# Four-head attention layer: logits row spread over partitions by DMA, mask built beside the first batch, one clock for all batches

## The chip, the cores and the metric

The kernel runs on one core of one Trainium2 chip. The time is the device time of one execution in microseconds. Before the change it is 3026.18 us (median of 3 runs, 3023.26 to 3026.87). The profiled execution has a span of 3030.3 us.

## What is computed

32 graphs (batches) of 512 nodes with 256 features share one 512 x 512 adjacency matrix. Four layers follow one another, each on the normed input and added to it. Cut to what matters here, with the four-head layer in full:

```
for layer in 0..3:
    h = max(layernorm(x), 0);  x = x + gat(h)

layers 0, 1:  Wh = h @ W;  e[i,j] = leaky(s_i[i] + s_j[j]);  masked softmax over j;  att @ Wh
layer 2 (four heads of 64 features):
    Wh = (h @ W).reshape(B, N, 4, 64)
    e[i,j,h] = leaky(s_src[i,h] + s_dst[j,h]), alpha = 0.2, masked by adj
    alpha = softmax over j;  out[i,h,:] = sum_j alpha[i,j,h] Wh[j,h,:];  elu
layer 3:  mlp1 -> unmasked gat of width 512 -> mlp2 -> masked gat of width 256, with residuals
```

The kernel uses exp(leaky(a + b)) = exp(b) exp(alpha a) max(R[i], T[j]) with R and T exponentials of one node each, and what depends on the row i alone drops out of the softmax. So the unnormed weights of a head are, transposed, w[j, i] = max(R[i], T[j]) x mask[j, i]. T is a column per partition; R must stand as a row of 512 on every partition.

## The kernel before

All 32 batches are unrolled. Four streams (`NS = 4`) work on batches b, b+1, b+2, b+3 side by side; stream i takes batches i, i+4, and so on (`stream`, L709). Each batch is a generator that yields a due time wherever it may be interrupted; the loop at L722 always advances the stream with the earliest due time. `after_us` (L62) makes the due time: the stream's time, plus `STRETCH` times the matmul cycles of this step, plus `SLOW` (1.5) times the microseconds given, times `pace`. Streams start `LEAD = 75` due microseconds apart. A fifth generator, `setup` (L213), is advanced every 4 due microseconds and prepares the weights of later layers. The due times fix the order in which instructions are written; a list scheduler may still move independent instructions of an engine past one another, unless `tc.keep_in_program_order` holds one in place. After that each engine's queue runs in order.

For the last four batches `pace` is 1.15, 1.025, 0.9 and 0.775 (L712), so that the streams, which run 75 due microseconds apart, are drawn together at the end.

`weights` (L335) makes w for one head: four TensorE transposes (L72) of R's column, broadcast to 128 x 128, against the identity fill a PSUM bank with R on every partition; then four DVE instructions (L343) of 128 x 512 take max(R, T) x mask into the SBUF tile w. [...] `layer2` (L424) makes the values v of all heads, begins head 0, and then for each head begins the next one (`begin`, L443), yields, and aggregates: 16 matmuls of 65 columns (L458), a reciprocal and a multiplication into the tile ya (L461). Layers 0, 1 and 3 use `weights` once each.

Layer 3's unmasked attention is done by sorting (`sort_attend`, L527): rows are scattered to DRAM by GpSimd (L571), read back in order by SyncE (L578), summed, written as a table (L611, L612) and gathered (L619). Only the last batch uses `attend` instead, by matmuls. SyncE's queue thus carries the sort's reads and writes, the loads of x (L89) and the outputs (L678).

The mask (L190 to L202) is made before the first batch: adj is loaded (1 MB), DVE compares it (L191), GpSimd sets the diagonal (L192), TensorE turns it with 16 transposes and ACT copies it to bf16.

Of the kernel before, what the change touches and what calls it, by code (L numbers as in the profile page):

```python
# [19 lines left out]
FP = mybir.dt.float32  # L20
# [4 lines left out]
OP = mybir.AluOpType  # L25
AX = mybir.AxisListType

EPS = 1.0e-5
P = 128
# [2 lines left out]
TINY = 1.0e-30  # L32
CYCLES = 2400.0


@with_exitstack
def fast(ctx, tc, flag, x, adj, w0, a0, w1, a1, w2, a2, mlp1_w, mlp1_b, mlp2_w, mlp2_b,
         w_fc, a_fc, w_hand, a_hand, out):
    nc = tc.nc
    B, N, F = x.shape  # L40
    NT = N // P
# [3 lines left out]
    NH = a2.shape[0]  # L45
    D = F // NH
    NS = 4
    LEAD = 75.0
    SLOW = 1.5
    STRETCH = 2.0  # L50

    const = ctx.enter_context(tc.tile_pool(name="const", bufs=1))
    work = ctx.enter_context(tc.tile_pool(name="work", bufs=2))
    psum = ctx.enter_context(tc.tile_pool(name="psum", bufs=1, space=bass.MemoryType.PSUM))
    dram = ctx.enter_context(tc.tile_pool(name="dram", bufs=1, space=bass.MemoryType.DRAM))

    turn = [0]
    begun = [0.0]
    spent = [0.0]
    pace = [1.0] * NS  # L60

    def after_us(us):  # L62

        return begun[0] + pace[turn[0]] * (STRETCH * spent[0] / CYCLES + SLOW * us)

    def matmul(p, w, x, **flags):
        spent[0] += 4 * max(x.shape[-1], P)
        nc.tensor.matmul(p, w, x, **flags)  # L68

    def transpose(p, x, i):  # L70
        spent[0] += 2 * P
        nc.tensor.transpose(p, x, i)  # L72

    def bank():
        return psum.tile([P, N], FP, tag=f"b{turn[0]}", name="b", bufs=8 // NS)
# [3 lines left out]
    ident = const.tile([P, P], FP, name="ident")  # L79
# [23 lines left out]
    def scale_a(t, alpha):  # L103
        nc.vector.tensor_scalar_mul(t[:, :, 1:2], t[:, :, 0:1], alpha - 1.0)
        nc.vector.tensor_scalar_mul(t[:, :, 2:3], t[:, :, 2:3], 1.0 - alpha)
# [25 lines left out]
    def finish_w(fetched, alpha):  # L131
        t, a_cols = fetched

        def block(k, f):
            c = f * P + (3 if f * P >= F else 0)
            return t[:, k, c:c + P]

        scale_a(a_cols, alpha)
        for k in range(t.shape[1]):
            project(t[:, k, F:F + 3], block, k, a_cols)  # L140
            yield
# [4 lines left out]
    adj_sb = work.tile([P, NT, N], I32, tag="w", name="adj", bufs=4)  # L146
# [10 lines left out]
    for h in range(NH):  # L157
        t, r = divmod(h * D, P)
# [27 lines left out]
    for _ in finish_w(fetched0, 0.2):  # L186
        pass


    own = work.tile([P, NT, N], FP, tag="w", name="own", bufs=4)  # L190
    nc.vector.tensor_scalar(own, adj_sb, 0.0, None, op0=OP.is_gt)  # L191
    nc.gpsimd.affine_select(  # L192
        out=own, in_=own, pattern=[[P, NT], [-1, N]], base=0, channel_multiplier=1,
        compare_op=OP.not_equal, fill=1.0,
    )
    maskT = const.tile([P, NT, N], BF, name="maskT")
    for j in range(NT):
        turn[0] = j % NS
        p = bank()
        for t in range(NT):  # L200
            transpose(p[:, t * P:(t + 1) * P], own[:, t, j * P:(j + 1) * P], ident)
        nc.scalar.copy(maskT[:, j, :], p)  # L202

    before = const.tile([P, P], FP, name="before")
    after = const.tile([P, P], FP, name="after")
    band = const.tile([P, 2 * N - P], BF, name="band")
    differ = const.tile([P, 2], FP, name="differ")
# [4 lines left out]

    def setup():  # L213

        yield from finish_w(fetched1, 0.01)


        nc.vector.tensor_reduce(differ[:, 0:1], adj_sb, AX.XY, OP.min)
        nc.vector.tensor_scalar(differ[:, 0:1], differ[:, 0:1], 0.0, None, op0=OP.is_lt)
        least = small([1], "rden")  # L220
        nc.vector.tensor_reduce(least, diag, AX.X, OP.min)
        nc.vector.tensor_scalar(differ[:, 1:2], least, 0.0, None, op0=OP.is_le)
        nc.vector.tensor_copy(W2[:, :, :, :D], raw2.rearrange("p k (h d) -> p k h d", d=D))
        nc.vector.tensor_scalar_mul(A2v[:, :, 1:2], A2v[:, :, 0:1], -0.8)
        nc.vector.tensor_scalar_mul(A2v[:, :, 2:3], A2v[:, :, 2:3], 0.8)
        for k in range(KF):
            project(W2[:, k, :, D:], lambda k, f: raw2[:, k, f * P:(f + 1) * P], k, A2)
            yield
        yield from finish_w(fetched3, 0.2)

        for tri, sign in ((before, 1), (after, -1)):
            nc.vector.memset(tri, 1.0)
            nc.gpsimd.affine_select(
                out=tri, in_=tri, pattern=[[sign, P]], base=0, channel_multiplier=-sign,
                compare_op=OP.is_gt, fill=0.0,
            )
        ties = work.tile([P, 2 * N - P], FP, tag="w", name="ties", bufs=4)
        nc.vector.memset(ties, TINY)
        nc.gpsimd.affine_select(
            out=ties, in_=ties, pattern=[[-1, 2 * N - P]], base=N - P, channel_multiplier=1,  # L240
            compare_op=OP.is_gt, fill=0.0,
        )
        nc.vector.tensor_copy(band, ties)
        yield
        yield from finish_w(fetched4, 0.2)
# [3 lines left out]
    def small(shape, name):  # L249
        return work.tile([P] + shape, FP, tag=name, name=name, bufs=2 * NS)  # L250
# [81 lines left out]
            yield after_us(0.9 if f == ft - 1 else 0)  # L332
        return o

    def weights(r_col, t_col, masked=True):  # L335

        r = bank()
        for t in range(NT):
            transpose(r[:, t * P:(t + 1) * P], r_col(t).to_broadcast([P, P]), ident)
        wt = work.tile([P, NT, N], FP, tag="w", name="w", bufs=4)  # L340
        for j in range(NT):
            if masked:
                nc.vector.scalar_tensor_tensor(  # L343
                    wt[:, j, :], r, t_col(j), maskT[:, j, :], op0=OP.max, op1=OP.mult
                )
            else:
                nc.vector.tensor_scalar(wt[:, j, :], r, t_col(j), None, op0=OP.max)  # L347
        return wt

    def pair(tag="y"):  # L350
        return work.tile([P, 2, F], FP, tag=tag, name=tag, bufs=3)
# [72 lines left out]
    def layer2(xt, xn, rs, when):  # L424
        hT = yield from turned(xn, when)
        v = work.tile([P, NT, NH, CH], FP, tag="v", name="v2", bufs=4)
        for t in range(NT):
            ps = bank()
            for k in range(KF):
                matmul(  # L430
                    ps[:, :NH * CH], hT[:, k, t * P:(t + 1) * P], W2[:, k, :, :], start=(k == 0), stop=(k == KF - 1)
                )
            pv = ps[:, :NH * CH].rearrange("p (h c) -> p h c", c=CH)
            nc.scalar.activation(v[:, t, :, D:], pv[:, :, D:], AF.Exp, scale=rs[:, t:t + 1])
            nc.vector.scalar_tensor_tensor(
                v[:, t, :, :D], pv[:, :, :D], rs[:, t:t + 1], v[:, t, :, D:D + 1].to_broadcast([P, NH, D]),
                op0=OP.mult, op1=OP.mult,
            )
            yield after_us(0 if t + 1 < NT else 1)
        ya = work.tile([P, NT, F], FP, tag="y4", name="y4", bufs=2)  # L440
        wts = []

        def begin(h):  # L443
            wts.append(weights(lambda t: v[:, t, h, D + 2:D + 3], lambda j: v[:, j, h, D + 1:D + 2]))
            return after_us(3.2)

        when = begin(0)
        note(v.rearrange("p t h c -> p (t h) c")[:, :, D:])
        yield after_us(1)
        for h in range(NH):  # L450
            last = when
            if h + 1 < NH:
                when = begin(h + 1)
            yield last
            wt = wts[h]
            p = bank()
            for t in range(NT):
                aggregate(p[:, t * (D + 1):(t + 1) * (D + 1)], wt, t, lambda j: v[:, j, h, :D + 1])  # L458
            pv = p[:, :NT * (D + 1)].rearrange("p (t c) -> p t c", c=D + 1)
            r = reciprocal(pv[:, :, D:])  # L460
            nc.vector.tensor_tensor(  # L461
                ya[:, :, h * D:(h + 1) * D], pv[:, :, :D], r.to_broadcast([P, NT, D]), op=OP.mult
            )
            if h % 2:
                c = slice((h - 1) * D, (h + 1) * D)
                y = ya[:, :, c]
                q = pair("q").rearrange("p a (b f) -> p (a b) f", f=2 * D)
                nc.scalar.activation(q, y, AF.Exp)
                nc.scalar.activation(y, y, AF.Relu)
                add_elu(xt[:, :, c], y, q)  # L470
            yield after_us(0)
        xn, rs = new_xn(), small([NT], "rs")
        for t0 in range(0, NT, 2):
            norm(xt, xn, rs, t0, False)
        yield after_us(7)
        return xn, rs, after_us(2)
# [231 lines left out]

    def stream(first):  # L709
        for b in range(first, B, NS):  # L710

            if b >= B - NS:  # L712
                pace[first] = 1.15 - (NS - B + b) / (2 * NS)
            yield from batch(b)


# [1 line left out]
    ready = {i: i * LEAD for i in range(NS)}  # L718
    streams = [stream(i) for i in range(NS)]
    early = setup()  # L720
    ready[NS] = 0.0
    while ready:  # L722
        i = min(ready, key=ready.get)
        if i == NS:
# [20 lines left out]
    p = bank()  # L745
# [437 lines left out]
```

## Time and profile before

| Quantity | Value |
|---|---|
| time, median of 3 | 3026.18 us |
| TensorE busy (matmul / weight load) | 2924.8 / 2368.3 us |
| DVE, ACT, GpSimd busy | 2269.9, 1489.6, 470.2 us |
| transposes that write R in layers 0 to 3 (b <- ident, v) | 896, mean 274 ns |
| w instructions on DVE (L343) | 896, mean 743 ns |
| mean DMA rate | 81 GB/s |
| first output sent / output of batch 27 sent | 289.9 / 2749.5 us |

Busy time is the time in which an engine has an instruction running. TensorE's matmuls are pipelined: a record is longer than the distance from one start to the next, so a queue of them is measured by its starts. A wait line names an engine's instruction, what released it, the total, the number of times, and the longest. "SPq" is SyncE's queue, which issues transfers. A stretch is a window in microseconds from the span's start.

### The profile page before, as it was taken

The numbers are of one execution on the slowest core, as the hardware profiler recorded it, in microseconds if no ns is written. First come the engines' busy times: TensorE is split into PE (matmuls) and PEld (weight loads), VectorE is DVE, ScalarE is ACT, GpSimd is POOL, SyncE is SP. The second block draws the span as 40 slices with busy tenths as digits, with TensorE's granted clock in tenths as the row PEclk, the third lists the DMA queues.
The fourth block names the chain that finished last, engine by engine and source line by source line (L and its number), as shares of the span: only waits on it lengthen the run. The fifth ranks groups of instructions, "written<-read, shape, count | busy, mean of one in ns | idle before, by whom it ended". The sixth has DMA issues, their size and how long they took to land. (4 is left out here: it accounts for less than half of the span.)

```text
span 3030.3 us, 43501 instructions
## 1 busy us (share of the span) xinstructions
PE 2924.8 (97%) x15529; PEld 2368.3 (78%) x15529; DVE 2269.9 (75%) x5674; ACT 1489.6 (49%) x3758; POOL 470.2 (16%) x509
## 2 busy tenths in 40 slices
PE   7999999999999999999999999999999999999897
PEld 5787887877788877788877788877888877788665
DVE  4588778777877777777778777877877877767664
ACT  3444455554455554455554455554455554454445
POOL 0011111101111201112111111101111111111111
PEclk8999999999999999999999999999999999999999
DMA  3022223222223222223232223222223222212220
GB/s 91 1 88 87 75 74 102 83 90 88 74 74 102 84 89 83 80 74 102 78 95 82 81 74 102 83 90 91 71 74 102 89 84 87 74 52 82 84 97 29
DMA packets 178685, 245.46 MB, mean 81 GB/s; under 512 B 15328, under 2 KB 153886, under 8 KB 178464
## 3 DMA queue, kind: packets, MB, share of 16 engines
q1 hardware_dynamic: 148704, 144.32, 14.9%
q0 software_dynamic: 29760, 98.30, 9.8%
q8 instruction: 125, 2.05, 0.3%
q14 instruction: 96, 0.79, 0.1%
HBM read 127.46 MB, written 115.12 MB: 80 GB/s over the span
## 5 line engine op out<-in xcount | busy, mean ns | idle before, releaser
L68 PE MATMUL b<-v,w 128*128 128x257 f32 (+1 forms) x7232 | 1225.5, 322 | 22.0 <-DVE w L343 8.6
L68 PEld LDWEIGHTS b<-v,w 128*128 128x128 f32 x7232 | 1054.2, 192 | 186.7 <-issue 51.7
L343 DVE SCALAR_TENSOR_TENSOR w<-b,v,maskT 128x512 f32<-128x512 f32 x896 | 635.7, 743 | 13.3 <-PE b L72 10.5
L68 PE MATMUL b<-WFC,oT 128*128 128x256 f32 (+1 forms) x2048 | 491.5, 380 | 0.8 <-ACT v L311 0.5
L68 PEld LDWEIGHTS b<-WFC,oT 128*128 128x128 f32 x2048 | 373.6, 189 | 50.8 <-issue 1.0
L68 PE MATMUL b<-W,hT 128*128 128x259 f32 (+1 forms) x1536 | 389.1, 391 | 9.8 <-DVE v L315 8.6
L68 PEld LDWEIGHTS b<-W,hT 128*128 128x128 f32 x1536 | 282.8, 192 | 60.2 <-DVE v L315 11.0
L571 POOL DMA_INDIRECT order<-v,at x248 | 251.1, 1013 | 462.7 <-DVE seen L298 139.9
L68 PE MATMUL b<-hT,WM 128*128 128x512 f32 x512 | 251.9, 598 | 8.2 <-ACT hT L282 7.8
L359 DVE RECIPROCAL rden<-b 128x1 f32<-128x1 f32 (+1 forms) x516 | 80.2, 163 | 233.6 <-PE b L68 230.6
L677 POOL TENSOR_TENSOR x<-x,y 128x512 f32<-128x512 f32 x64 | 81.2, 1269 | 1077.3 <-ACT y L675 980.8
L619 POOL DMA_INDIRECT g<-table,at x124 | 122.5, 988 | 790.8 <-ACT y L639 287.1
L68 PE MATMUL b<-oT,WM 128*128 128x512 f32 x512 | 232.8, 597 | 0.0
L261 DVE BATCH_NORM_STATS2 st<-x 128x6 f32<-128x256 f32 x512 | 193.2, 409 | 5.6 <-DMA x<-in_x_dram 2.7
L331 ACT ACTIVATE oT<-b,bias 128x512 f32<-128x512 f32 x128 | 87.5, 686 | 216.6 <-PE b L68 216.4
L384 DVE TENSOR_TENSOR y<-q,y 128x512 f32<-128x512 f32 x192 | 132.5, 691 | 67.1 <-ACT q L383 48.2
L72 PEld LDWEIGHTS b<-ident,xn 128*128 128x128 f32 x1024 | 125.9, 142 | 69.9 <-DVE xn L272 23.6
L493 ACT ACTIVATE v<-b,ends 128x256 f32<-128x256 f32 x256 | 120.3, 470 | 122.2 <-PE b L68 115.6
L72 PE MATMUL b<-ident,xn 128*128 128x128 f32 x1024 | 159.7, 278 | 20.4 <-DVE xn L272 8.7
L282 ACT ACTIVATE hT<-b 128x512 f32<-128x512 f32 x256 | 150.2, 593 | 40.7 <-PE b L72 39.6
L68 PEld LDWEIGHTS b<-oT,WM 128*128 128x128 f32 x512 | 95.3, 191 | 93.5 <-issue 91.4
L638 ACT ACTIVATE q<-g,rden 128x512 f32<-128x512 f32 x124 | 89.5, 722 | 145.9 <-DVE rden L359 142.7
(139 smaller groups left out, 3735.0 us busy)
## 6 DMA issues: line engine op xcount, KB each, us to landing
table<-sums SPq DMA_DIRECT2D x62, 1032.0 KB
sums<-order SPq DMA_DIRECT2D x62, 516.0 KB
x<-in_x_dram SPq DMA_DIRECT2D x32, 512.0 KB
out_dram<-x SPq DMA_DIRECT2D x64, 256.0 KB
sums<-order SPq DMA_DIRECT2D x62, 129.0 KB
order<-v,at POOLq DMA_INDIRECT x248, 2.5
g<-table,at POOLq DMA_INDIRECT x124, 4.5
adj<-in_adj_dram SPq DMA_DIRECT2D x1, 1024.0 KB
```

The costliest lines, as they stand in the source:

```text
L68: nc.tensor.matmul(p, w, x, **flags)
L72: nc.tensor.transpose(p, x, i)
L261: nc.vector.bn_stats(st[:, i, :], xt[:, t0 + i, :])
L282: nc.scalar.activation(hT[:, :, t0 * P:(t0 + 2) * P], p.rearrange("p (k n) -> p k n", k=KF), AF.Relu)
L331: nc.scalar.activation(o[:, f, :], p, AF.Relu, bias=bias[:, f:f + 1])
L343: nc.vector.scalar_tensor_tensor(wt[:, j, :], r, t_col(j), maskT[:, j, :], op0=OP.max, op1=OP.mult)
L384: nc.vector.tensor_tensor(r, q, r, op=OP.add)
L493: nc.scalar.activation(halves[c][:, t, :F], ps[:, :F], AF.Copy, scale=ends[:, t, 0:1])
L571: nc.gpsimd.indirect_dma_start(out=orders[c], out_offset=bass.IndirectOffsetOnAxis(ap=at[:, 0, t:t + 1], axis=0), in_=halves[c][:, t, :], ...
L619: nc.gpsimd.indirect_dma_start(out=g, out_offset=None, in_=table, in_offset=bass.IndirectOffsetOnAxis(ap=at[:, 1, t:t + 1], axis=0),)
L638: nc.scalar.activation(q, z, AF.Exp, scale=rd)
L677: nc.gpsimd.tensor_tensor(xr, xr, y, op=OP.add)
```

## The change

Three things are done at once.

In layer 2, only head 0 gets its R by broadcast transposes. For heads 1 to 3, four transposes of v's R columns give a 4 x 512 row tile in PSUM, ACT copies it to SBUF (a buffer of the tag q), SyncE writes it to a DRAM tile, and three reads with a partition broadcast put a row on all 128 partitions of an SBUF tile `spread` (two buffers for all streams). `weights` takes such a tile as `r` and holds the head's first w in program order. To make room, ya has one buffer instead of two. The due time after head 0 begins grows from 1 to 3.

The mask moves into `setup`, whose start moves from 0 to 7.5 due microseconds; its first transpose and the reduction of adj (L218) are held in program order.

`pace` is dropped: the last four batches have the same due times as all others.

```diff
     def after_us(us):
-        return begun[0] + pace[turn[0]] * (STRETCH * spent[0] / CYCLES + SLOW * us)
+        return begun[0] + STRETCH * spent[0] / CYCLES + SLOW * us
...
-    own = work.tile([P, NT, N], FP, tag="w", name="own", bufs=4)
-    nc.vector.tensor_scalar(own, adj_sb, 0.0, None, op0=OP.is_gt)
-    nc.gpsimd.affine_select(
...
     def setup():
+        own = work.tile([P, NT, N], FP, tag="w", name="own", bufs=4)
+        nc.vector.tensor_scalar(own, adj_sb, 0.0, None, op0=OP.is_gt)
+        nc.gpsimd.affine_select(
...
+        for j in range(NT):
+            turn[0] = NS - 1 - j % (NS - 1)
+            p = bank()
+            for t in range(NT):
+                transpose(p[:, t * P:(t + 1) * P], own[:, t, j * P:(j + 1) * P], ident, j + t == 0)
+            nc.scalar.copy(maskT[:, j, :], p)
+        turn[0] = NS - 1
+        yield
         yield from finish_w(fetched1, 0.01)
-        nc.vector.tensor_reduce(differ[:, 0:1], adj_sb, AX.XY, OP.min)
+        tc.keep_in_program_order(nc.vector.tensor_reduce(differ[:, 0:1], adj_sb, AX.XY, OP.min))
...
-    def weights(r_col, t_col, masked=True):
-        r = bank()
-        for t in range(NT):
-            transpose(r[:, t * P:(t + 1) * P], r_col(t).to_broadcast([P, P]), ident)
+    def weights(r_col, t_col, masked=True, r=None):
+        landed = r is not None
+        if not landed:
+            r = bank()
+            for t in range(NT):
+                transpose(r[:, t * P:(t + 1) * P], r_col(t).to_broadcast([P, P]), ident)
...
+                if landed and j == 0:
+                    tc.keep_in_program_order(w)
...
-        ya = work.tile([P, NT, F], FP, tag="y4", name="y4", bufs=2)
+        ya = work.tile([P, NT, F], FP, tag="y4", name="y4", bufs=1)
...
+        p = bank()
+        for t in range(NT):
+            transpose(p[:NH, t * P:(t + 1) * P], v[:, t, :, D + 2], ident)
+        row = pair("q").rearrange("p a f -> p (a f)")[:NH, :]
+        nc.scalar.copy(row, p[:NH, :])
+        row_d = dram.tile([NH, N], FP, tag="row", name="row", bufs=3)
+        nc.sync.dma_start(row_d, row)
+        spread = [None]
+        for h in range(1, NH):
+            r = work.tile([P, N], FP, tag="spread", name="spread", bufs=2)
+            nc.sync.dma_start(r, row_d[h, :].partition_broadcast(P))
+            spread.append(r)
         when = begin(0)
...
-        yield after_us(1)
+        yield after_us(3)
...
-            if b >= B - NS:
-                pace[first] = 1.15 - (NS - B + b) / (2 * NS)
...
-    ready[NS] = 0.0
+    ready[NS] = 7.5
```

More of the change, by code (lines that the diff above doesn't have):

```diff
@@ L59, in fast @@
     spent = [0.0]
-    pace = [1.0] * NS
     def after_us(us):
-        return begun[0] + pace[turn[0]] * (STRETCH * spent[0] / CYCLES + SLOW * us)
+        return begun[0] + STRETCH * spent[0] / CYCLES + SLOW * us
     def matmul(p, w, x, **flags):
@@ L68, in matmul, with transpose @@
         nc.tensor.matmul(p, w, x, **flags)
-    def transpose(p, x, i):
+    def transpose(p, x, i, tied=False):
         spent[0] += 2 * P
-        nc.tensor.transpose(p, x, i)
+        instruction = nc.tensor.transpose(p, x, i)
+        if tied:
+            tc.keep_in_program_order(instruction)
     def bank():
@@ L187, in fast @@
         pass
-    own = work.tile([P, NT, N], FP, tag="w", name="own", bufs=4)
-    nc.vector.tensor_scalar(own, adj_sb, 0.0, None, op0=OP.is_gt)
-    nc.gpsimd.affine_select(
-        out=own, in_=own, pattern=[[P, NT], [-1, N]], base=0, channel_multiplier=1,
-        compare_op=OP.not_equal, fill=1.0,
-    )
-    maskT = const.tile([P, NT, N], BF, name="maskT")
-    for j in range(NT):
-        turn[0] = j % NS
-        p = bank()
-        for t in range(NT):
-            transpose(p[:, t * P:(t + 1) * P], own[:, t, j * P:(j + 1) * P], ident)
-        nc.scalar.copy(maskT[:, j, :], p)
+    maskT = const.tile([P, NT, N], BF, name="maskT")
     before = const.tile([P, P], FP, name="before")
@@ L213, in setup @@
     def setup():
+        own = work.tile([P, NT, N], FP, tag="w", name="own", bufs=4)
+        nc.vector.tensor_scalar(own, adj_sb, 0.0, None, op0=OP.is_gt)
+        nc.gpsimd.affine_select(
+            out=own, in_=own, pattern=[[P, NT], [-1, N]], base=0, channel_multiplier=1,
+            compare_op=OP.not_equal, fill=1.0,
+        )
+        for j in range(NT):
[6 more added lines that the diff above has]
+        yield
         yield from finish_w(fetched1, 0.01)
-        nc.vector.tensor_reduce(differ[:, 0:1], adj_sb, AX.XY, OP.min)
+        tc.keep_in_program_order(nc.vector.tensor_reduce(differ[:, 0:1], adj_sb, AX.XY, OP.min))
         nc.vector.tensor_scalar(differ[:, 0:1], differ[:, 0:1], 0.0, None, op0=OP.is_lt)
@@ L333, in linear_t @@
         return o
-    def weights(r_col, t_col, masked=True):
-        r = bank()
-        for t in range(NT):
-            transpose(r[:, t * P:(t + 1) * P], r_col(t).to_broadcast([P, P]), ident)
+    def weights(r_col, t_col, masked=True, r=None):
[4 more added lines that the diff above has]
+                transpose(r[:, t * P:(t + 1) * P], r_col(t).to_broadcast([P, P]), ident)
         wt = work.tile([P, NT, N], FP, tag="w", name="w", bufs=4)
@@ L342, in weights @@
             if masked:
-                nc.vector.scalar_tensor_tensor(
+                w = nc.vector.scalar_tensor_tensor(
                     wt[:, j, :], r, t_col(j), maskT[:, j, :], op0=OP.max, op1=OP.mult
                 )
+                if landed and j == 0:
+                    tc.keep_in_program_order(w)
             else:
@@ L439, in layer2 @@
             yield after_us(0 if t + 1 < NT else 1)
-        ya = work.tile([P, NT, F], FP, tag="y4", name="y4", bufs=2)
+        ya = work.tile([P, NT, F], FP, tag="y4", name="y4", bufs=1)
         wts = []
         def begin(h):
-            wts.append(weights(lambda t: v[:, t, h, D + 2:D + 3], lambda j: v[:, j, h, D + 1:D + 2]))
-            return after_us(3.2)
+            wts.append(
+                weights(
+                    lambda t: v[:, t, h, D + 2:D + 3], lambda j: v[:, j, h, D + 1:D + 2], r=spread[h] if h else None
+                )
+            )
+            return after_us(3.2)
+        p = bank()
[10 more added lines that the diff above has]
+            spread.append(r)
         when = begin(0)
         note(v.rearrange("p t h c -> p (t h) c")[:, :, D:])
-        yield after_us(1)
+        yield after_us(3)
         for h in range(NH):
```

## The prediction

> **What bounds the kernel now.** I began with the busy shares, then asked who makes TensorE wait in the steady part, then read the slices and stretches for the two ends. The page, shares and slices (tenths busy in 40 slices of 76 us):
>
> ```profile
> PE 2924.8 (97%) x15529; PEld 2368.3 (78%) x15529; DVE 2269.9 (75%) x5674; ACT 1489.6 (49%) x3758; POOL 470.2 (16%) x509
> ...
> PE   7999999999999999999999999999999999999897
> ...
> DMA  3022223222223222223232223222223222212220
> ```
>
> TensorE is busy in 97% of the span, with DVE at 75%, and only the first slice and the last three fall off. [...] I checked the waits of the PE queue from 400 to 2400 us (who waited for what: total, times, longest):
>
> ```profile
> PE b L72 <- DVE v L315: 10.1, 11, 1.0
> PE b L68 <- DVE v L315: 7.1, 11, 1.0
> PE b L72 <- DVE xn L272: 4.6, 17, 0.3
> PE b L68 <- ACT hT L282: 3.4, 5, 0.7
> PE b L68 <- DVE w L343: 3.3, 6, 0.6
> ```
>
> All its waits come to about 31 us in 2000. In the middle, TensorE's queue is never empty: an instruction taken from it is time taken from the span, unless a new wait eats it. The outputs say the same: batch 0 is sent at 289.9 us and batch 22 at 2287.0, so a batch takes 90.8 us. What a transpose costs is in the order of time of TensorE:
>
> ```profile
> 1129.22 0.60 PE L72 MATMUL b<-ident,v 128*128 128x128 f32 x4
> 1129.66 1.04 PE L68 MATMUL b<-W,hT 128*128 128x259 f32 x4
> 1130.54 0.60 PE L72 MATMUL b<-ident,v 128*128 128x128 f32 x4
> 1130.97 0.60 PE L72 MATMUL b<-ident,ends 128*128 128x128 f32 x4
> ```
>
> Four transposes hold the queue from 1130.54 to 1130.97: 0.43 to 0.44 us, 0.109 each, although one record lasts 273 ns. The two ends, in stretches (length, then busy us of PE, PEld, DVE, ACT, POOL, then clock):
>
> ```profile
> 400.00:2400.00 2000.00, 1968.27 (x10578) 1604.65 (x10577) 1563.43 (x3900) 1018.12 (x2580) 328.48 (x353) 1.00 0.26 85
> 2749.00:2817.00 68.00, 64.61 (x367) 53.15 (x366) 52.81 (x131) 31.35 (x84) 13.12 (x15) 1.00 0.29 94
> 2817.00:2884.00 67.00, 58.82 (x292) 45.15 (x291) 41.40 (x96) 25.28 (x56) 10.12 (x12) 0.92 0.22 72
> 2884.00:2952.00 68.00, 60.65 (x258) 43.02 (x257) 39.70 (x88) 31.73 (x69) 9.11 (x9) 0.95 0.31 101
> 2952.00:3020.00 68.00, 61.40 (x271) 44.99 (x269) 33.59 (x74) 37.87 (x83) 7.29 (x6) 1.00 0.07 24
> ```
>
> In the steady part TensorE starts 5.3 matmuls per us; from 2749 (batch 27 leaves) to 3020, 1188 in 271 us, 4.4 per us. The tail wastes some 40 us.
>
> [...] here 273 ns per record, but 109 ns from start to start, and the second is what a queued one costs. [...] the small row scatters (order) land in 2.5 us. [...] 128x512 scalar_tensor_tensor takes 684 ns from PSUM (L690, L674) and 684 ns from SBUF (L377).
>
> **The change, part by part.**
>
> *R of heads 1 to 3 by DMA.* Per batch, 12 transposes go (heads 1 to 3, four each) and four come (one set for all heads; their output is four rows, but the moving operand is still 128 columns of ident, so I price them at the same 0.109; the 128x1 transpose at the end has a record of 270 ns too). Net 8 x 0.109 = 0.87 us a batch, x 32 = **-27.8 us** of TensorE, nearly all where it is saturated.
>
> The w instructions read R from SBUF: 743 ns before (L343); L634, with two SBUF sources and a pointer scalar as here, takes 748. No change[...]. ACT gains one copy of four rows, 0.58 us (L545), x 32 = 18.5 us on an engine at 49%: hidden. DMA gains 3 x 256 KB a batch, 25 MB on 245 MB, at a share of 26%: hidden but for latency.
>
> The new wait is DVE's. The first w of heads 1 to 3 is pinned in program order, so where R hasn't landed DVE stands, and behind it the other streams' norms, sort scans and w. How long is the chain? Transposes 0.6, ACT copy 0.6 and about 0.5 in its queue, the row written 2.5 (as the order scatters), then the spread. Reads of half a megabyte show 4.6 us from issue to first use (sums<-order, 1155.87 to 1160.49) and 4.1 (1160.20 to 1164.26); half the bytes should be 3 to 4. Total 7.2 to 8.2 us. How much time is there? The planner puts 3 x 1.5 = 4.5 due us and 1.7 for eight transposes between, 6.2; a batch is 301 due us (its yields added up) and 4 x 90.8 = 363 real, so 1.2 real per due: 7.5 us. Head 1 is thus on the edge; heads 2 and 3 come one aggregate (about 7 due us) later each. Head 3's tile needs the buffer of head 1 (two for all streams) and so its transfer follows head 1's w, with two heads' time to land. The transfers stand in the SP queue:
>
> ```profile
> 1116.80 0.38 SPq L89 DMA_DIRECT2D x<-in_x_dram  x1
> 1155.87 0.57 SPq L578 DMA_DIRECT2D sums<-order  x1
> 1156.49 0.61 SPq L579 DMA_DIRECT2D sums<-order  x1
> ```
>
> Layer 2's w of this batch run on DVE from 1130.7; SP has nothing between 1117 and 1156, so it is free unless the sort's read is queued ahead. Cost: 0 if R is always there, 31 x 2 = 62 if each batch loses 2 us outright on TensorE. DVE has 22% free and TensorE a queue of ready work, so I take **+6**. The wait before head 1 grows by 2 x 1.5 = 3 due us; a batch becomes 303 due us, which only interleaves otherwise.
>
> *y4 on one buffer, a third user of q.* Layer 2 takes 57 of 75 due us between streams, so two never hold y4 at once; q has three buffers, one held some 4 us per 91. Nothing.
>
> *Mask beside the first batch.* At the start TensorE waits for own until 13.35 and turns the mask until 16.6, and batch 0's xn, ready at 7.9, follows. The 2.3 us reduction of adj (11.29) also stands on DVE ahead of W0's last columns (13.49). Afterwards half of batch 0 can turn before the mask and the reduction is pinned behind. But w needs the mask (last copy 17.5) and began at 23.7: between 0 and 5 us; I take **-2**.
>
> *Same clock for the last four.* With pace the last batches are due to end at 2453, 2490, 2528 and 2536 (yields added up), bunched; without, at 2425, 2500, 2575 and 2613. So four streams run for 75 due us after batch 27, then three, two, and one for 38. The start shows these stages mirrored, by the first Exp of each batch's layer 0: one stream took 19.2 to 76.8 (57.5 us, setup included), two 65.3, three 73.6, four 88.6. So 88.6 + 73.6 + 65.3 + 57.5 x 38/75 (29) = 257 us, where the old tail took 270.5 (2749.5 to 3020): **-14**. Faster [...]: layer 1's to layer 2's values of batch 0 took 18.0 us for 37 due, which makes 19 of the 29. Slower if the sort's transfers, hidden before, stand bare. Range -35 to +25.
>
> Sum: -27.8 + 6 - 2 - 14 = -38; 3026 - 38 = **2988**.
>
> **The rivals.**
> 1. *R comes late* (slower). The read waits in SP's queue behind the sort's read, which waits up to 140 us for its scatters, and the pinned w stops DVE. For: 1.2 MB of traffic in that neighbourhood, a margin near zero for head 1. Against: SP's gap above, and DVE's slack. 2 us a batch on TensorE gives 62 in place of 6: 3044; worse if head 3 is caught too.
> 2. *The tail loses.* The bunching was worth more than the bare stages: +25 in place of -14, so 3027, no change. For: the last stream stands alone at the end, latency-bound. Against: the old tail's 4.4 matmuls per us.
> 3. *All goes well.* No stall, lone stages fast, tail -35: 3026 - 28 - 2 - 35 = 2961.
>
> **How the numbers follow.** Forecast (2970 to 3015) 0.52; late R (3032 and up) 0.15; lost tail (3015 to 3032) 0.13; all well (under 2970) 0.20. The low end, 2955, keeps most of the last; the high end, 3032, keeps the lost tail; what lies outside is late R and the far end of case 3, 0.2. Under 3020 lies the forecast, case 3 and a third of the lost tail: 0.77; within 6 us of 3026: 0.07; above: 0.16.
>
> **What would show it.** Transposes from v should fall from 896 to 640, the batch interval from 90.8 to about 90.1. A DVE wait for spread should be small in total (under 60 us) and no new releaser should appear in PE's list. Outputs of batches 28 to 31 should come apart by about 74, 65 and 29 us instead of crowding after 2917. The mask's transposes should stand behind part of batch 0's. Wrong if DVE waits for spread by microseconds in each batch, if SP issues the spread after the sort's reads, or if the last output is over 260 us behind batch 27's.

## The result, and the profile after

The changed kernel takes 2957.98 us (median of 4, 2957.28 to 2962.42) against 3025.83 us beside it: 0.978 times, 95% interval 0.9763 to 0.9797, some 68 us less where 38 were forecast. It lies 3 us inside the low end of the range. The profiled spans, 3030.3 and 2956.8 us, differ by 73.5.

The page after, shares and slices:

```profile
PE 2870.2 (97%) x15273; PEld 2335.9 (79%) x15273; DVE 2270.1 (77%) x5674; ACT 1493.6 (51%) x3790; POOL 496.9 (17%) x509
...
PE   7999999999999999999999999999999999999998
...
DMA  3022233232232332232222232222232222332230
```

TensorE has 256 matmuls less (15,529 to 15,273) and stays the bound at 97%. What is new is the end: the last three slices, 8, 9 and 7 before, are full but for the last. DMA's busy share rises in a few slices and stays at three tenths. The PE queue's waits from 400 to 2400 us, all of them:

```profile
PE b L70 <- DVE v L316: 18.9, 22, 1.0
PE b L70 <- DVE xn L273: 12.4, 22, 0.8
```

31.3 us, as before (about 31); no wait for a w or for spread has come up. The w instructions by where R is read from, a PSUM bank (b) or the tile spread (after the bar: busy us, mean ns of one, then the idle time before them and its releaser):

```profile
L346 DVE SCALAR_TENSOR_TENSOR w<-b,v,maskT 128x512 f32<-128x512 f32 x512 | 369.8, 743 | 4.9 <-PE b L70 4.9
...
L346 DVE SCALAR_TENSOR_TENSOR w<-spread,v,maskT 128x512 f32<-128x512 f32 x384 | 269.4, 741 | 0.5 <-DMA spread<-row 0.5
```

One takes 741 ns with R in SBUF and 743 with R in PSUM. DVE waited 0.5 us for spread in the whole run, once.

Where the 73.5 us of the spans lie can be read from the times at which outputs are sent. Batch 0 leaves at 285.8 instead of 289.9 (4.1 us). From batch 0 to 22 a batch takes 89.35 us instead of 90.78. Batch 27 leaves at 2700.5 instead of 2749.5, so 44.9 us come from between, and the rest, some 24 us, from after it.

### The profile page after: what moved, and what is told of

Same layout as the page of the kernel before. It is cut to its first block, busy times and chain, and to the rows that moved or that the text cites. A ratio compares the mean times of both kernels' runs of the same rounds, so it can differ in the third digit from the quotient of the medians.

```text
span 2956.8 us, 43040 instructions
## 1 busy us (share of the span) xinstructions
PE 2870.2 (97%) x15273; PEld 2335.9 (79%) x15273; DVE 2270.1 (77%) x5674; ACT 1493.6 (51%) x3790; POOL 496.9 (17%) x509
## 4 chain that ended last, share of the span: by engine, by line
PE 85%; DVE 9%; ACT 3%; issue 2%; DMA 1%; POOL 0%; SPq 0%; POOLq 0%; ACTq 0%; DVEq 0%
PE b L66 77%; PE b L70 8%; DVE st L262 2%; DVE xn L273 1%; DVE xn L269 1%; DVE y L697 1%; DVE v L316 1%; ACT rs L265 1%; DVE y L389 0%; DVE w L346 0%; DVE mv L263 0%; DVE x L421 0%; DVE tot L633 0%; ACT q L388 0%; DMA sums<-order 0%
## 5 line engine op out<-in xcount | busy, mean ns | idle before, releaser
L66 PE MATMUL b<-v,w 128*128 128x65 f32 (+1 forms) x7232 | 1218.1, 321 | 9.7 <-DVE w L346 8.2
L66 PE MATMUL b<-WFC,oT 128*128 128x256 f32 (+1 forms) x2048 | 499.7, 381 | 3.0 <-ACT ends L515 3.0
L346 DVE SCALAR_TENSOR_TENSOR w<-b,v,maskT 128x512 f32<-128x512 f32 x512 | 369.8, 743 | 4.9 <-PE b L70 4.9
L594 POOL DMA_INDIRECT order<-v,at x248 | 280.3, 1130 | 467.5 <-DVE w L346 159.8
L346 DVE SCALAR_TENSOR_TENSOR w<-spread,v,maskT 128x512 f32<-128x512 f32 x384 | 269.4, 741 | 0.5 <-DMA spread<-row 0.5
L389 DVE TENSOR_TENSOR y<-q,y 128x512 f32<-128x512 f32 x192 | 132.6, 691 | 59.9 <-ACT q L388 58.5
L66 PEld LDWEIGHTS b<-oT,WM 128*128 128x128 f32 x512 | 97.7, 191 | 96.0 <-issue 92.7
```

Of the source, the lines that this page charges most:

```text
L346: w = nc.vector.scalar_tensor_tensor(wt[:, j, :], r, t_col(j), maskT[:, j, :], op0=OP.max, op1=OP.mult)
L389: nc.vector.tensor_tensor(r, q, r, op=OP.add)
L594: nc.gpsimd.indirect_dma_start(out=orders[c], out_offset=bass.IndirectOffsetOnAxis(ap=at[:, 0, t:t + 1], axis=0), in_=halves[c][:, t, :], ...
```

## The experiments

Each ratio is to the kernel before, run beside the variant, with its 95% interval. "Interval" without more is the mean distance between outputs from batch 0 to batch 22; it and the spans come from one profiled execution of each variant.

### The three parts apart

**The common clock alone** (kernel before):

```diff
-            if b >= B - NS:
-                pace[first] = 1.15 - (NS - B + b) / (2 * NS)
```

> The kernel before with one edit: the last four batches keep the common clock (R by transposes, mask first, as before). My theory (the end gains by itself, because the bunched streams wasted TensorE): 25 to 32 us faster, about 2996; outputs of batches 0 to 23 at the same times as before within 1 us, the last output about 251 us behind that of batch 27. Rival (the end gains only because layer 2 got shorter and its waits fell away): within 8 us of before.

Measured: 3006.14 us, 0.9916 of before (0.9902 to 0.9929); 25.2 us in the spans. Batch 23 leaves at 2375.9 (before 2378.5), batch 27 at 2739.0 (2749.5). So of the 25 us, 2.6 are there by batch 23, 8 were lost by the batches up to 27, which still ran beside the first of the last four, and 15 after batch 27. My theory holds: the end gains by itself. Two of its details do not: the earlier outputs move by more than 1 us, and the last output comes 260 us behind batch 27's, not 251. Each half of an output is ready when GpSimd adds y to x. The first halves of batches 27 to 31 after the whole change (start, duration, idle before):

```profile
2699.19 1.29 POOL L700 TENSOR_TENSOR x<-x,y 128x512 f32<-128x512 f32 x1
...
2786.96 1.26 POOL L700 TENSOR_TENSOR x<-x,y 128x512 f32<-128x512 f32 x1 [41.24 <-ACT y L698]
...
2860.99 1.27 POOL L700 TENSOR_TENSOR x<-x,y 128x512 f32<-128x512 f32 x1 [28.95 <-ACT y L698]
...
2922.01 1.27 POOL L700 TENSOR_TENSOR x<-x,y 128x512 f32<-128x512 f32 x1 [44.55 <-ACT y L698]
...
2944.58 1.27 POOL L700 TENSOR_TENSOR x<-x,y 128x512 f32<-128x512 f32 x1 [12.94 <-ACT y L698]
```

The steps are 87.8, 74.0, 61.0 and 22.6 us, where the mirrored start gave 88.6, 73.6, 65.3 and 29. With the clock alone the outputs come 89.3, 81.5, 61.1 and 22.6 us apart, so the second step agrees only with layer 2 changed as well.

**The mask alone** (kernel before): own, affine_select and the 16 transposes move into setup, the first of these transposes and the reduction of adj are pinned in program order, `ready[NS] = 7.5`:

```diff
-    own = work.tile([P, NT, N], FP, tag="w", name="own", bufs=4)
...
+        own = work.tile([P, NT, N], FP, tag="w", name="own", bufs=4)
...
-        nc.vector.tensor_reduce(differ[:, 0:1], adj_sb, AX.XY, OP.min)
+        tc.keep_in_program_order(nc.vector.tensor_reduce(differ[:, 0:1], adj_sb, AX.XY, OP.min))
...
-    ready[NS] = 0.0
+    ready[NS] = 7.5
```

> The kernel before with one edit: the mask made in setup beside batch 0, with the reduction of adj pinned behind it. My theory: batch 0 leaves about 4 us earlier and all later outputs keep that lead, so 2 to 5 us faster, about 3022. Rival (the start is swallowed by the streams' stagger, and batch 0's lead in the changed kernel came from layer 2): no change within 1 us.

Measured: 3024.14 us, 0.9978 (0.9969 to 0.9987), so 4 to 9 us less. Batch 0 leaves at 285.3 (4.6 us earlier), batch 25 is 5.1 us earlier, and batch 27, at 2747.2, only 2.3: the drawn-together end loses half of the lead. Beside the common clock it is kept: the next run differs from the one with the common clock alone by the mask only, and its span is 5.8 us shorter (3005.1 to 2999.3). In TensorE's order of time of the run with the mask alone, batch 0 has turned all its xn, and begun its values (two matmuls of W), before the mask starts:

```profile
12.41 1.97 PE L72 MATMUL b<-ident,xn 128*128 128x128 f32 x8 [0.80 <-DVE W L122]
14.21 1.23 PE L68 MATMUL b<-W,hT 128*128 128x259 f32 x2
15.24 3.33 PE L72 MATMUL b<-ident,own 128*128 128x128 f32 x16
```

**R by transposes again, mask and common clock kept** (changed kernel; the row's transposes, its copy and its transfers are left out, y4 has two buffers, the due time is 1):

```diff
-                    ... r=spread[h] if h else None
+                    ... r=None
-        yield after_us(3)
+        yield after_us(1)
```

> The changed kernel with the first part undone: R of heads 1 to 3 by transposes into PSUM again, y4 on two buffers, due time 1 after head 0; mask and common clock stay. My theory (the R part is worth what the steady interval shows, 1.43 us a batch): 38 to 46 us slower than the changed kernel, about 3000, with the interval back at 90.8. Rival (the shorter interval comes from the due times or the end's clock): interval stays near 89.4 and the time under 2975.

Measured: 3000.65 us, 0.9897 (0.9882 to 0.9913), interval 90.77. As my theory said, the R part alone brings the shorter interval; it is worth 42.5 us of the spans (2999.3 to 2956.8). By the outputs, 8.7 of them come after batch 27.

### What in the R part brings 42 us

**Eight transposes put back, R still by DMA:**

```diff
+        for h in (1, 2):
+            for t in range(NT):
+                nc.tensor.transpose(
+                    p[:, t * P:(t + 1) * P], v[:, t, h, D + 2:D + 3].to_broadcast([P, P]), ident
+                )
         for t in range(NT):
             transpose(p[:NH, t * P:(t + 1) * P], v[:, t, :, D + 2], ident)
```

> The changed kernel with eight more transposes a batch, written into the row's PSUM bank ahead of the four that are used and overwritten by them; their result is not read, and due times don't count them. It puts TensorE's work back to that of before, with R still coming by DMA. Theory A (the gain is TensorE's time alone, 0.87 to 0.96 us a batch plus what their waits cost): 28 to 46 us slower than the changed kernel, interval 90.2 to 90.8. Rival B (the gain is that DVE no longer holds a PSUM bank while it makes w, and reads SBUF): under 10 us slower, interval under 89.7.

Measured: 2986.07 us, 0.9853 (0.9837 to 0.9868), interval 90.25, span 2985.0. The 256 transposes are worth 28.2 us of the span, 0.110 each, and 0.90 us of the interval. The PE queue's waits in this run, 400 to 2400 us:

```profile
PE b L70 <- DVE v L316: 18.9, 22, 1.0
PE b L70 <- DVE xn L273: 12.4, 22, 0.8
PE b L66 <- ACT v L312: 0.8, 1, 0.8
```

The two that matter are those of the changed kernel to the tenth, so in the middle nothing but TensorE's work has moved. Theory A holds for 28 of 42 us; 14 remain. The run also prices the narrow transposes that write the row (four columns, 128*4). In TensorE's order of time the eight that were put back stand next to four narrow and four full ones:

```profile
1034.86 1.03 PE L461 MATMUL b<-ident,v 128*128 128x128 f32 x8
1035.73 1.04 PE L70 MATMUL b<-ident,v 128*4 128x128 f32 x8
```

The second line begins 0.87 us after the first, and what follows it begins at 1036.61, 0.88 later. So a narrow one costs the queue as much as a full one, as priced.

**R by transposes under the new due times** (heads 1 to 3 not counted in the due times, four for the row counted, 3 after head 0; the row's own transposes, copy and transfers are left out, y4 has two buffers):

```diff
+                (transpose if counted else nc.tensor.transpose)(
...
+        spent[0] += NT * 2 * P
         when = begin(0)
...
+        yield after_us(3)
```

> The changed kernel with R of heads 1 to 3 by transposes into PSUM, but with the due times of the changed kernel kept to the cycle (3 after head 0, four transposes counted for the row, those of heads 1 to 3 not counted). Against the run with eight extra transposes it differs only in where DVE reads R and in the PSUM bank held meanwhile. Theory O (what the R part gave beyond the transposes, some 14 us, is the order of the streams' work under the new due times): interval 90.1 to 90.4, time 2983 to 2991. Theory P (it is the PSUM bank that DVE no longer holds): interval 90.7 to 90.9, time 2998 to 3003.

Measured: 2990.43 us, 0.9874 (0.9857 to 0.9891), interval 90.39, span 2989.5. Theory O takes most: the due times alone bring the span from 2999.3 to 2989.5, 9.8 us, with TensorE's instructions unchanged. By the ratios it is 7 us, and their intervals just overlap, so the size is not firm. The 9.8 us are not a steady gain alone: batch 0 leaves 8.1 us later than in the run before, each batch then gains some 0.4 us, batch 27 leaves 1.9 us earlier, and 7.9 us come after it, most of them in the step from batch 28 to 29 (74.8 us in place of 81.5; the changed kernel has 74.0). TensorE's waits (78 and 80 us in all) and mean clock (0.994 in both) are the same; what shrinks is its busy time, from 2910.9 to 2899.1 us. Why the same instructions take less in this order was not found out. The other 4.5 us of the span, to 2985.0, would be the place of R: the PSUM bank, the source, or the pin, the copy and the buffer of y4, in which the two runs also differ. The intervals of these two ratios overlap. Theory P, which forecast 2998 to 3003, doesn't account for the 14 us by itself, and is neither shown nor excluded for 4.5. So the span goes 2999.3, 2989.5, 2985.0, 2956.8: order 9.8, place of R 4.5, transposes 28.2.

### How near the edge the new wait is

**Due time 1 after head 0** (changed kernel):

```diff
-        yield after_us(3)
+        yield after_us(1)
```

> The changed kernel with due time 1 in place of 3 after head 0. The chain row, DRAM, spread then has about 3.6 us less ahead of head 1's first w. My prediction's step (head 1 is on the edge with 7.5 us): DVE would now wait for spread 2 to 4 us in each batch, 60 us or more in total, and the time rises by 5 to 30 us. Rival (the transfer had time to spare, or the scheduler places head 1's w behind other work anyway): waits under 15 us, and only the order of the streams changes the time, by up to 15 us either way.

Measured: 3149.29 us, 1.0391 (1.0377 to 1.0406): 191 us slower than the changed kernel. Both theories are wrong about the size, and mine about the cause as well. DVE's wait for spread came to 12.0 us in 16 waits, under the 15 of the rival. Due time 1 is not bad as such: with R by transposes, all of them counted in the due times, it ran at 90.77 a batch. One of the bad places, in DVE's order of time, then TensorE's, then the stretch from 1020 to 1040 us (length, then busy PE, PEld, DVE, ACT, POOL, then clock):

```profile
1014.19 0.74 DVE L346 SCALAR_TENSOR_TENSOR w<-spread,v,maskT 128x512 f32<-128x512 f32 x1
...
1021.39 0.43 DVE L614 TENSOR_TENSOR sums<-sums 128x258 f32<-128x258 f32 x1 [6.36 <-DMA sums<-order]
...
1025.52 0.75 DVE L346 SCALAR_TENSOR_TENSOR w<-spread,v,maskT 128x512 f32<-128x512 f32 x1
...
1026.79 2.73 DVE L346 SCALAR_TENSOR_TENSOR w<-spread,v,maskT 128x512 f32<-128x512 f32 x4
```

```profile
1019.08 1.88 PE L66 MATMUL b<-oT,WM 128*128 128x512 f32 x4
1026.33 7.09 PE L66 MATMUL b<-v,w 128*128 128x65 f32 x32 [5.37 <-DVE w L346]
1033.21 3.72 PE L66 MATMUL b<-oT,WM 128*128 128x512 f32 x4
```

```profile
1020.00:1040.00 20.00, 14.63 (x61) 11.47 (x60) 10.14 (x26) 4.91 (x11) 0.00 (x0) 0.66 0.16 53
```

R of head 2 has been there since its first w, but its last w and the four of head 3 stand in DVE's queue behind the sum of another stream's sort, which waits 6.4 us for its read, and behind 4 us of other work that piled up meanwhile. TensorE then waits 5.4 us for that w, and its clock falls: 0.66 on the mean of these 20 us, 32 aggregate matmuls taking 7.1 us where the same 32 took 3.68 at a clock of 1.00 in the kernel before (1134.01), and four matmuls of 512 columns taking 3.72 us after the stall where they took 1.88 ahead of it. How long a gap does that was not shown: the kernel before runs at a clock of 0.50 from 2648.3 to 2651.7, right behind a gap of 2.0 us (to 2648.13), and the changed kernel keeps 1.00 after one of 2.3 us (to 2846.94). The mean clock of the run is 0.967 against 0.994. In the changed kernel the same w are through before the sum starts:

```profile
1049.69 0.74 DVE L346 SCALAR_TENSOR_TENSOR w<-spread,v,maskT 128x512 f32<-128x512 f32 x1
1053.35 0.41 DVE L614 TENSOR_TENSOR sums<-sums 128x258 f32<-128x258 f32 x1
```

**No pin, at due time 3:**

```diff
-                if landed and j == 0:
-                    tc.keep_in_program_order(w)
```

> The changed kernel without the hold in program order on the first w of heads 1 to 3. If the pin costs DVE idle time that reaches TensorE: faster by 2 us or more. If the pin matters for the order (without it w moves ahead and DVE waits for spread): waits for spread appear and the time rises. If neither: within 3 us.

Measured: 2958.30 us, 0.9763 (0.975 to 0.9777): no difference from the changed kernel that these runs show. DVE waited for spread 0.7 us, once. At this due time the pin costs and brings nothing.

**No pin, at due time 1:**

```diff
-                if landed and j == 0:
-                    tc.keep_in_program_order(w)
...
-        yield after_us(3)
+        yield after_us(1)
```

> The kernel with due time 1 after head 0 (3149 us), without the hold in program order on the first w of heads 1 to 3. Theory D (the pin stops DVE's queue at a w whose R the scheduler counts as not landed, and the rest of the order goes wrong behind it): back to an interval under 91 and a time under 3010. Theory C (DVE's queue has the sort's first sum, which waits for its read, ahead of layer 2's last w; the pin is not the cause): stays over 3120.

Measured: 3022.36 us, 0.9981 (0.9972 to 0.9989), interval 90.9. This is between the two theories, nearer to D: the pin accounts for 127 of the 191 us, but 64 remain against 2958.3. DVE's wait for spread is the same with and without the pin:

```profile
DVE w L346 <- DMA spread<-row: 12.3, 16, 1.6
```

So the pin doesn't cost by DVE standing at an R that isn't there (12 us in all, either way). What goes with it is DVE's wait for the sort's reads, 63.8 us in 17 waits with the pin and 10.2 in 15 without, so it costs by the queue orders that the scheduler makes around it. TensorE's waits fall from 164 to 93 us, and the mean clock rises from 0.967 to 0.990.

**The sort's sums four units (6 due us) later, at due time 1:**

```diff
-        sort = after_us(11)
+        sort = after_us(15)
```

> The kernel with due time 1 after head 0 (3149 us), with the sort's sums written 6 due us later (15 in place of 11 in the wait ahead of them). Theory C: the sums no longer stand ahead of layer 2's last w, the wait of DVE for the sort's read falls from 64 us to under 30 and the time falls by 60 us or more. Theory D, or the short wait as such: within 30 us of 3149.

Measured: 3135.80 us, 1.0354 (1.0336 to 1.0371), 13 us less.

```profile
DVE sums L614 <- DMA sums<-order: 28.0, 7, 5.1
```

The wait named by theory C fell from 63.8 to 28.0 us, as it should, and the time hardly moved. That does not dispose of theory C, because the edit removed the waits that TensorE didn't feel. Seven of TensorE's long stalls fall together with such a wait in either run: 36.8 us of stall with the due time alone, 37.0 with the sums later. One of them with the sums later, on DVE and then on TensorE:

```profile
927.66 0.43 DVE L614 TENSOR_TENSOR sums<-sums 128x258 f32<-128x258 f32 x1 [5.09 <-DMA sums<-order]
929.41 1.11 PE L70 MATMUL b<-ident,y 128*128 128x128 f32 x4 [6.37 <-DVE y L389]
```

Here it is not a w that stands behind the sum but the tile y (L389) that TensorE has to turn next; in the run with the due time alone the same pair stands at 921.33 and 923.08. Other stalls come with no wait for data at all: at 1026.34 in this run TensorE waits 2.4 us for a w while DVE works without a gap. So both kinds of queue order are in the loss, and this run doesn't part them.

**Due time 5:**

```diff
-        yield after_us(3)
+        yield after_us(5)
```

> The changed kernel with due time 5 in place of 3 after head 0. If 3 is a threshold (R is there, more only delays layer 2): 2955 to 2965. If the order of the streams is what counts and is brittle: off by more than 10 us in either direction.

Measured: 3032.50 us, 1.0020 (1.0011 to 1.0029). More time for the transfer is 74 us slower. So 3 is no threshold after which R is there; the time as a function of this one number runs 3149, 2958, 3032 for 1, 3 and 5. DVE never waits for spread in this run. TensorE's waits are up from 77 to 98 us, the largest share being eleven waits, 25.6 us in all, for a norm's factor (rs, L265); with due time 1 there were two. The mean clock of the run is 0.985 against 0.994. The order is what counts, and it is brittle.

### Head 0 by DMA as well

**A wait of five ahead of head 0, of one after it:**

```diff
-        spread = [None]
-        for h in range(1, NH):
+        spread = []
+        for h in range(NH):
...
+        yield after_us(5)
         when = begin(0)
...
-        yield after_us(3)
+        yield after_us(1)
```

> The changed kernel with head 0's R spread by DMA as well (four transposes a batch fewer, a wait of 5 due us ahead of head 0, 1 after it). By the measured price of a transpose (28 us for 256) the TensorE time falls by 14 us: about 2944, interval 88.9. Rival: the new wait ahead of head 0, with two spread buffers for four heads, makes DVE wait for spread, or the new order of the streams costs as much: 2958 or more.

Measured: 3156.12 us, 1.0416 (1.0402 to 1.043). TensorE's largest wait, and DVE's largest for a transfer, in this run:

```profile
PE b L66 <- DVE w L346: 57.6, 33, 5.2
```

```profile
DVE sums L615 <- DMA sums<-order: 93.7, 36, 7.1
```

The rival is right about the time. Of its two causes the first is out, since no wait of DVE for spread shows up at all; the new order is left.

**Five ahead of head 0, three after it:**

```diff
-        spread = [None]
-        for h in range(1, NH):
+        spread = []
+        for h in range(NH):
...
+        yield after_us(5)
```

> Head 0's R by DMA as well (3156 us with 5 due us ahead of head 0 and 1 after it), with 3 after it. If the 1 was what made it slow, as in the run with due time 1: back to the order of the changed kernel and 14 us less TensorE, about 2944 to 2950. If two buffers for four heads are too few or the order stays bad: over 3000.

Measured: 3060.65 us, 1.0117 (1.0096 to 1.0139). 96 us better than with 1 and still 103 slower than the changed kernel. DVE waited 16.1 us for spread in 18 waits. TensorE's 14 us were not had with these due times and two buffers; which of the two stands in the way was not separated. No run was faster than the changed kernel.

## Why the prediction was right, and where its sizes were off

The mechanism was right, and the sum was off by 30 us, by the spans 35. Of these, 6 are the wait for R that didn't come, 15 are mask and clock, which gave 31 and not 16, and 14 are a term that the prediction had put at nothing. The result lies in the range by 3 us only. The low end was drawn for rival 3, no stall and 37 us from mask and tail, which made 2961; the result came near it by another sum. That it stayed inside is luck as far as the order of the queues goes, which nothing in the prediction bounded.

**The bound** was right: TensorE's work comes off one to one. Priced at 0.109 us a transpose from its start-to-start times, the term -27.8 measured -28.2. The record's 273 ns would have promised 70.

**DVE's wait for R, +6,** measured nothing: 0.5 us. The chain was priced well, and the time too short. In the changed kernel (SyncE's queue, then DVE):

```profile
1025.46 0.27 SPq L464 DMA_DIRECT2D row<-q  x1
1027.35 10.34 SPq L468 DMA_DIRECT2D spread<-row  x3
```

```profile
1034.60 2.73 DVE L346 SCALAR_TENSOR_TENSOR w<-spread,v,maskT 128x512 f32<-128x512 f32 x4
```

The row takes 1.9 us from its issue to the issue of the first spread, which waits for it to land (1.4 to 3.3 over the 32 batches). The first w of head 1 comes 9.1 us after the row is sent, in 29 of 32 batches 9.1 to 10.0, where I had allowed 7.5 for the whole chain, the transposes and the copy ahead of the row included. With due time 1 the chain itself can be read: DVE's 16 waits for spread are all at head 1's first w, and there R has landed 4.7 to 6.5 us after the row was sent, near the 5.5 to 6.5 that the prediction gave to row and spread. So due time 3 left about 3 us to spare, and due time 1 nothing. The sort's reads come after the spreads in SyncE's queue (1047.13), as forecast; rival 1 did not occur.

**The order, not in the sum:** -14.3 us with the place of R. "A batch becomes 303 due us, which only interleaves otherwise" is the step that failed. The due times alone were worth 9.8 us here, 7.9 of them after batch 27, and one step to either side costs 74 and 191. I had put the risk of the changed layer 2 into a late transfer; it lay in the orders of the queues, which no row of the profile before could price.

**The mask, -2,** measured -4 to -9 by itself and 5.8 beside the common clock, by the mechanism named. I had thought that half of batch 0 would turn before the mask; all of it did.

**The clock, -14,** measured -21 to -30 (interval of the run alone). The stages after batch 27, which the term prices, gave 15 of 14, in part by chance: three streams took 81.5 us and not 73.6, the last two stages 84 and not 94. With layer 2 changed they gave 24. Left out of the term were the batches before: in the profile before, batches 25 to 27 follow at 92.7 to 95.6 us, and 8 us of that were the pace's doing. Rival 2, the lost tail, is out: the last stage alone took 22.6 us.

Sum in spans: mask and clock 31.0, order 9.8, place of R 4.5, transposes 28.2, together 73.5.

What stays open: why these orders cost what they do. The traces show where a good part of it lies. TensorE's waits, added up, and what its mean clock takes from the span:

| Kernel | Span, us | TensorE's waits, us | (1 - mean clock) x span, us |
|---|---|---|---|
| changed kernel | 2956.8 | 77 | 18 |
| due time 1 | 3147.6 | 164 | 104 |
| due time 1, no pin | 3015.5 | 93 | 30 |
| due time 1, sums later | 3133.5 | 144 | 110 |
| due time 5 | 3031.9 | 98 | 45 |

With due time 1, waits and clock together explain some 160 of the 191 us (13 us stand in both columns), with due time 5 some 48 of 75. In each of these four runs 25 to 30 us lie in neither. They are in the time in which TensorE counts as busy at full clock, and they stay unexplained, as do the 12 us of busy time that the due times alone saved. Why the scheduler's order lets TensorE run dry at due times 1 and 5 and not at 3 was not read to its end either.

## What to carry to other kernels

Where one engine's queue is never empty, price what you take from it by the distance between starts, and expect it back in full; moving such work to DMA was worth 28 us here although it lengthened the chain from v to w. Ask of a transfer in a software-interleaved kernel not only whether it lands in time but what it does to the order of the queues: a due time changed by 2 cost up to 191 us with 12 us of wait for the data itself. Then look at the bound engine's own waits and its clock; they show the loss even where no wait for the new data does. And when streams run staggered, their start, read backwards, tells about how long they will take to run out; with the clock alone the sum came within about 2 us, the single stages only within 8.

## What the runs showed that was not expected

A stall of TensorE of 5.4 us was paid about twice. In the stretch from 1020 to 1040 us, with a mean granted clock of 0.66, the matmuls run at about half their pace until 1036.72, 10.4 us after the stall's end: the 32 take 7.1 us in place of 3.7, and the four behind them 3.7 in place of 1.9, another 5.2 us lost.

And the transpose of four columns (a weight load of 128 x 4) costs TensorE's queue as much as one of 128: 0.88 us for four of each, beside 0.87 for eight full ones. An output of four rows in place of 128 saved nothing.
